# A step of the expert mixture is issued behind a deferred projection instead of behind the scores

## The chip, the cores and the metric

The kernel runs on one core of a Trainium2 chip. The metric is the device time of one execution in microseconds (us). The engines are TensorE (PE: matmuls; PEld: its weight loads), VectorE (DVE), ScalarE (ACT), GpSimd (POOL) and SyncE (SP, which only issues transfers). Each works through its own queue in order.

## The reference, cut to what matters

A layer with eight sequences of 512 tokens and 512 features. With `xn` the layer norm of `x`:

```python
s = attention(xn)          # 16 heads, chunks of 128, decay masks, carried states,
                           # gate and group norm, then @ Wo
g = silu(moe(xn))          # 16 experts, the 4 best of each token, and a shared expert
return x + s * g
```

In `moe`, every token's result is the sum of four weighted expert rows and of the shared expert's row times a sigmoid.

## The kernel before, in words

The work is in three stages. First norms, routing, the shared expert and the attention of sequences 0 and 1; then the routed experts, whose rows go to a DRAM table `y_d`; then the attention of sequences 2 to 7 (`FIRST` = 2), beside which the expert rows are gathered and mixed. The change is in this last stage.

One sequence there (`sequence`, L857) goes through four groups of four heads. For each group, in the order of the code: `scores` (L703: states, scores, VectorE's masking `sc<-ps,dmask` L750), the key of the next but one group (`key`, L678: a matmul `pk`, silu `sk` on ScalarE, and on VectorE a shuffle and three products and sums, L671 to L675), `by_token` (L684: transposes of the next key), one or two tiles of the *deferred* projection of the sequence before (`project_tiles`), the query (`query`, L681: as the key, matmul `pq`), and `output` (L755: matmuls `po`, product L776). The projection `pw` (L817) is finished by `last` (L1350): VectorE multiplies `m` by `pw` out of PSUM (L1363), then GpSimd adds `x` (L1367, `xo<-xo,m`) and SP stores it. Group 0 finishes tiles 0 and 1 of the sequence before, group 1 tiles 2 and 3.

PSUM banks come by tag; `pw`, `pq`, `po` and odd value tiles share tag "d", which has two banks. So the second `pw` of a group waits for the bank of the first, which L1363 on VectorE empties.

Between these pieces stand calls of `step()`, which is `advance` (L1384). Each call moves every active mixture tile by one piece. A tile (`mixture`, L1312) consists of four gathers by GpSimd (L1325, one per call), the addition of the first two rows (L1331, GpSimd), the addition of the other two (L1334, GpSimd) with `m<-m,sg,yg` (L1336, VectorE), `m<-m,yg` (L1340, VectorE) and a silu (L1343, ScalarE). A new tile is begun in 5 of 11 calls. Tiles of sequences 0 and 1, whose attention result waits in DRAM, end in `last` at once (there L1363 reads `m<-m,s`). The GpSimd addition of `last` is held in a list `late` and issued by a later call:

```python
while late and late[0][0] + 1 < steps[0]:
    late.pop(0)[1]()
```

The order of each engine's queue is the order in which the code issues; `behind(engine)` pins the mixture's instructions to their place. The last sequence (7) has its own loop, `last_sequence` (L942), with its own calls of `step`.

Of the kernel before, what the change touches and what calls it, by code (L numbers as in the profile page):

```python
# [38 lines left out]
FIRST = 2  # L39
# [58 lines left out]
def tile_block(ctx: ExitStack, tc: tile.TileContext, a: dict, out: bass.AP):  # L98
# [496 lines left out]
    def load_xT(b, pool=None):  # L595
        xT = (pool or home(b)).tile([P, KC, N], F32, tag="xT", name=f"xT_{b}", bufs=1)
        nc.sync.dma_start(xT.rearrange("p k n -> p (k n)"), xT_d[b])
        xT_of[b] = xT
# [10 lines left out]
    def value(b, t):  # L609
        if t == 0:  # L610
            v_of[b] = att.tile([P, NC, D], F32, tag="v", name=f"v_{b}", bufs=2)
        pv = bank("d" if t % 2 else "m", f"pv_{b}_{t}")
        for k in range(KC):
            with on_pe():
                nc.tensor.matmul(  # L615
                    pv, lhsT=xT_of[b][:, k, t * P : (t + 1) * P], rhs=wv[:, k, :],
                    start=(k == 0), stop=(k == KC - 1))
            between[0]()
        nc.scalar.copy(v_of[b][:, t, :], pv)
# [4 lines left out]
    def gate_1(b):  # L624
        pg1 = bank("a", f"pg1_{b}")
        with on_pe():
            for k in range(KC):
                for t in range(NC):
                    nc.tensor.matmul(
                        pg1[t * Q : (t + 1) * Q, :P], lhsT=wg1[:, k, :],  # L630
                        rhs=xT_of[b][:, k, t * P : (t + 1) * P],
                        start=(k == 0), stop=(k == KC - 1))
        g1_of[b] = att.tile([P, P], F32, tag="tmp", name=f"g1_{b}", bufs=TMP)
        nc.scalar.copy(g1_of[b], pg1[:, :P])

    def gate_2(b, tiles=range(NC), banks="aaaa"):
        if 0 in tiles:
            on_of[b] = home(b).tile([P, G, N], F32, tag="on", name=f"on_{b}", bufs=1)
        g1 = g1_of[b]
        p2s = {t: bank(banks[t], f"p2_{b}_{t}") for t in tiles}  # L640
        with on_pe():
            for g in range(G):
                for t in tiles:
                    tq = slice(t * Q, (t + 1) * Q)
                    nc.tensor.matmul(
                        p2s[t][:, g * P : (g + 1) * P], lhsT=wg2[tq, g * P : (g + 1) * P],
                        rhs=g1[tq, :], start=True, stop=True)
        for t in tiles:
            nc.scalar.activation(
                on_of[b][:, :, t * P : (t + 1) * P],  # L650
                p2s[t].rearrange("p (g n) -> p g n", n=P), AF.Sigmoid)
        if NC - 1 in tiles:
            g1_of.pop(b)
# [24 lines left out]
    def key(b, g, ps=None):  # L678
        kT_of[g] = rotated(b, g, "k", wk, ps)

    def query(b, g):  # L681
        qT_of[g] = rotated(b, g, "q", wq)

    def by_token(b, g):  # L684

        if not kept:
            kept.append(bank("k", f"pk_{b}_{g}"))
        pk = kept[0]
        with on_pe():
            for c in range(NC - 1):  # L690
                nc.tensor.transpose(
                    pk[:, c * P : (c + 1) * P], kT_of[g][:, c * C : (c + 1) * C], ident)
        kd = scr[0].tile([P, NC - 1, HG, HD], F32, tag="kd", name=f"kd_{b}_{g}")
        by_chunk = pk[:, : (NC - 1) * P].rearrange("p (c h d) -> p c h d", c=NC - 1, d=HD)
        for j in range(HG):
            nc.scalar.activation(
                kd[:, :, j, :], by_chunk[:, :, j, :], AF.Copy,
                scale=dk[:, g * HG + j : g * HG + j + 1])
        kd_of[g] = pk[:, (NC - 1) * P :], kd
# [55 lines left out]
    def output(b, g):  # L755
        po = bank("d", f"po_{b}_{g}")
        st, qd, sc = st_of.pop(g), qd_of.pop(g), sc_of.pop(g)
        with on_pe():
            for c in range(1, NC):
                if carry:  # L760
                    nc.tensor.matmul(  # L761
                        po[:, c * C : (c + 1) * C], lhsT=st[:, c - 1, :], rhs=qd[:, c - 1, :],
                        start=(c == 1), stop=False)
                for j in range(0 if carry else HG):
                    hs = slice(j * HD, (j + 1) * HD)
                    nc.tensor.matmul(
                        po[hs, c * C : (c + 1) * C], lhsT=st[hs, c - 1, :], rhs=qd[hs, c - 1, :],
                        start=(c == 1), stop=False)
            for c in range(NC):
                for j in range(HG):  # L770
                    h = g * HG + j
                    nc.tensor.matmul(  # L772
                        po[j * HD : (j + 1) * HD, c * C : (c + 1) * C],
                        lhsT=v_of[b][:, c, h * HD : (h + 1) * HD],
                        rhs=sc[j][:, c], start=False, stop=(c == NC - 1))
        nc.vector.tensor_tensor(on_of[b][:, g, :], po, on_of[b][:, g, :], ALU.mult)  # L776
# [16 lines left out]
    def inverse(b):  # L793
        nc.vector.reciprocal(rs_of[b], rs_of[b])
# [18 lines left out]
    def project(b, t):  # L813
        pw = bank("d", f"pw_{b}_{t}")
        with on_pe():
            for g in range(G):
                nc.tensor.matmul(  # L817
                    pw, lhsT=on_of[b][:, g, t * P : (t + 1) * P], rhs=wo[:, g, :],
                    start=(g == 0), stop=(g == G - 1))
        return pw  # L820
# [36 lines left out]
    def sequence(b, step, projected, before=None, defer=False, also=lambda: None):  # L857


        n = b + 1  # L860

        def project_tiles(q, ts):
            if q is not None:
                for t in ts:
                    projected(q, t, project(q, t))


        fill = ([0], [1], [2], [3], [], [], [], [])
        for g in range(G):
            scores(b, g)  # L870
            late_step = b == 0 and g + 2 >= G
            if not late_step:
                step()
            if g + 2 < G:
                key(b, g + 2)
            else:
                value(n, 2 * (g - 2))
            if late_step:
                step()
            if g + 1 < G:  # L880
                by_token(b, g + 1)
            project_tiles(before, fill[2 * g])
            step()
            if g + 2 < G:
                query(b, g + 2)
                if g + 3 == G and n not in xT_of:
                    load_xT(n)
            if g + 2 == G:
                value(n, 1)
            if g == 0 and b not in on_of:  # L890
                gate_2(b)
            project_tiles(before, fill[2 * g + 1])
            if fill[2 * g + 1] == [NC - 1]:
                on_of.pop(before, None)
            output(b, g)
            if defer and g + 2 == G:
                gate_1(n)
            step()
        v_of.pop(b)
        if n == FIRST:  # L900
            for _ in range(4):
                next(filling)
            gate_1(n)
            next(filling, None)
            for e in range(E - LATE // 2, E):
                nc.sync.dma_start(wexp[:, e, :], a["experts"][:, e, :])
            squares(b)
            inverse(b)
            value(n, 3)
            normed(b)  # L910
            experts_of_blocks()
            return
        if defer:
            gate_2(n)
        value(n, 3)
        also()
        squares(b)
        step()
        inverse(b)
        key(n, 0)  # L920
        also()
        query(n, 0)
        normed(b)
        also()
        if not defer:
            step()
        key(n, 1)
        by_token(n, 0)
        if defer:
            step()  # L930
        query(n, 1)
        also()
        if not defer:
            gate_1(n)
            project_tiles(b, [0, 1])
            also()
            project_tiles(b, [2, 3])
            also()
            on_of.pop(b)
        step()  # L940
# [156 lines left out]
    along()  # L1097
    enter(0, along)
    sequence(0, along, spill, also=lambda: next(sorting, None))
    for _ in sorting:  # L1100
        pass
# [14 lines left out]
    next(filling)  # L1116
    between[0] = lambda: next(filling, None)
    sequence(1, lambda: None, spill)
    between[0] = lambda: None
    slot = slots[0]  # L1120
# [354 lines left out]
```

## Time and profile before

| | us |
|---|---|
| median of three timed runs | 1143.45 (1142.99 to 1148.04) |
| profiled execution, its own time | 1133.33 |
| its span, first to last instruction | 1131.5 |
| TensorE busy in the span | 1109.5 (98%) |
| VectorE busy | 753.3 (67%) |
| GpSimd busy | 446.2 (39%) |
| ScalarE busy | 427.6 (38%) |
| granted TensorE clock, mean | 0.997 of full speed |

The last stage runs from about 690 us to the end. Within it, sequences 3 to 6 have their first group from about 761, 835, 911 and 986 us on (the matmuls `ps` of L725). A timeline line gives start, duration, engine, line, operation, what is written and read, how many instructions were merged, and in brackets the idle time ahead of it and who ended it.

### The profile page before, as it was taken

The page shows a single profiled execution, that of the slowest core. Times are in us where ns is not written, and L with a number is a line of the kernel's source. Part 1 is how long each engine was busy: PE and PEld are TensorE (multiplying, and loading weights), DVE is VectorE, ACT ScalarE, POOL GpSimd, SP SyncE. Part 2 cuts the span into 40 slices and gives each one's busy share as a digit, 9 for nine tenths or more (in the row PEclk, how much of TensorE's full clock was granted, in tenths as well). Part 3 has the DMA queues.
Part 4 walks back from the last instruction along what each step waited for, and adds up shares of the span by engine and source line. Part 5 has one row for each costly group of instructions (what it writes and reads, how often), then busy time and mean ns, then how long its engine had stood idle before and what let it go on. Part 6 is the DMA issues. An engine that isn't in the chain of part 4 may idle for free. (4 is left out here: it accounts for less than half of the span.)

```text
span 1131.5 us, 21658 instructions
## 1 busy us (share of the span) xinstructions
PE 1109.5 (98%) x7838; PEld 682.4 (60%) x7838; DVE 753.3 (67%) x1608; ACT 427.6 (38%) x924; POOL 446.2 (39%) x430
## 2 busy tenths in 40 slices
PE   7999999999999999999999999999999999999998
PEld 4445554455577777777777885655645545546453
DVE  6357744998354455555555666978789597797774
ACT  3223525255433333333333442352432523423541
POOL 4312100200333333333332314836868858768111
PEclk9999999999999999999999999999999999999999
DMA  9895341192779999999999986714648537444012
GB/s 343 311 334 187 138 161 48 57 378 88 215 208 237 236 234 238 234 239 239 241 238 267 245 203 244 270 57 160 232 121 258 156 114 250 138 138 143 11 38 75
DMA packets 163932, 218.50 MB, mean 193 GB/s; under 512 B 89840, under 2 KB 99184, under 8 KB 161776
## 3 DMA queue, kind: packets, MB, share of 16 engines
q1 hardware_dynamic: 142704, 146.76, 42.0%
q0 software_dynamic: 21120, 70.34, 24.2%
q8 instruction: 64, 1.05, 0.4%
q14 instruction: 44, 0.36, 0.1%
HBM read 126.78 MB, written 72.43 MB: 176 GB/s over the span
## 5 line engine op out<-in xcount | busy, mean ns | idle before, releaser
L1226 PE MATMUL pgu<-xts,wst 128*128 128x256 f32 x896 | 202.6, 379 | 0.0
L1226 PEld LDWEIGHTS pgu<-xts,wst 128*128 128x128 f32 x896 | 170.1, 190 | 46.2 <-issue 13.4
L1325 POOL DMA_INDIRECT yg<-y_d,place x128 | 141.6, 1106 | 30.3 <-issue 19.1
L1157 POOL DMA_INDIRECT more<-xn_d,slot x69 | 65.5, 949 | 220.1 <-DVE w L1210 107.5
L1241 PE MATMUL py<-wexp,slb 128*128 x272 | 129.9, 593 | 0.0
L1245 DVE TENSOR_SCALAR y<-py,w 128x512 f32<-128x512 f32 x136 | 102.0, 751 | 41.8 <-PE py L1241 35.4
L615 PE MATMUL pv<-wv,xT 128*128 128x512 f32 x256 | 118.3, 603 | 0.0
L659 PE MATMUL pk<-xT,wk 128*128 128x512 f32 x256 | 118.1, 603 | 0.0
L659 PE MATMUL pq<-xT,wq 128*128 128x512 f32 x256 | 115.7, 593 | 0.5 <-PEq L1289 0.5
L1232 ACT ACTIVATE slb<-pgu 128x256 f32<-128x256 f32 (+1 forms) x80 | 28.1, 351 | 219.8 <-PE pgu L1226 216.4
L817 PE MATMUL pw<-wo,on 128*128 128x512 f32 x224 | 102.3, 604 | 5.1 <-DVE m L1363 4.3
L1157 POOL DMA_INDIRECT xg<-xn_d,slot x67 | 63.6, 949 | 98.8 <-DVE w L1210 44.0
L1233 DVE TENSOR_TENSOR slb<-slb,pgu 128x256 f32<-128x256 f32 (+1 forms) x80 | 30.5, 381 | 105.3 <-ACT slb L1232 101.4
L1367 POOL TENSOR_TENSOR xo<-xo,m 128x512 f32<-128x512 f32 x31 | 45.6, 1470 | 134.2 <-DVE m L1363 126.7
L1208 DVE COPY wst<-wexp 128x512 f32 x160 | 61.7, 426 | 41.0 <-DVE y L1245 24.5
L1190 ACT COPY xts<-pl 128x512 uint16<-128x512 uint16 x110 | 84.3, 769 | 0.3 <-DMA pl<-xg 0.2
L659 PEld LDWEIGHTS pq<-xT,wq 128*128 128x128 f32 x256 | 47.2, 190 | 54.4 <-issue 53.0
L750 DVE TENSOR_TENSOR sc<-ps,dmask 128x512 f32<-128x512 f32 x128 | 79.0, 676 | 0.9 <-PE ps L725 0.9
L659 PEld LDWEIGHTS pk<-xT,wk 128*128 128x128 f32 x256 | 46.2, 189 | 50.7 <-issue 48.3
L615 PEld LDWEIGHTS pv<-wv,xT 128*128 128x128 f32 x256 | 45.9, 190 | 49.7 <-issue 46.7
L817 PEld LDWEIGHTS pw<-wo,on 128*128 128x128 f32 x224 | 41.8, 193 | 55.5 <-issue 46.2
L734 ACT COPY blocked<-state 32x96 f32<-32x96 f32 x96 | 30.8, 321 | 83.0 <-DVE state L729 82.2
(193 smaller groups left out, 1728.4 us busy)
## 6 DMA issues: line engine op xcount, KB each, us to landing
y_d<-y SPq DMA_DIRECT2D x136, 256.0 KB
wexp<-in_experts SPq DMA_DIRECT2D x16, 768.0 KB
sh_d<-sh SPq DMA_DIRECT2D x32, 256.0 KB
xT<-xT_d SPq DMA_DIRECT2D x8, 1024.0 KB
m<-sh_d SPq DMA_DIRECT2D x32, 256.0 KB
xo<-in_x SPq DMA_DIRECT2D x32, 256.0 KB
out<-xo SPq DMA_DIRECT2D x31, 256.0 KB
x<-in_x SPq DMA_DIRECT2D x7, 1024.0 KB
```

The source lines that it names most:

```text
L615: nc.tensor.matmul(pv, lhsT=xT_of[b][:, k, t * P : (t + 1) * P], rhs=wv[:, k, :], start=(k == 0), stop=(k == KC - 1))
L659: nc.tensor.matmul(ps, lhsT=w[:, k, g * P : (g + 1) * P], rhs=xT_of[b][:, k, :], start=(k == 0), stop=(k == KC - 1))
L750: masked[:] = [nc.vector.tensor_tensor(s, pss[j].rearrange("p (c t) -> p c t", t=C), dmask[:, g * HG + j].unsqueeze(1).to_broadcast([P, NC ...
L817: nc.tensor.matmul(pw, lhsT=on_of[b][:, g, t * P : (t + 1) * P], rhs=wo[:, g, :], start=(g == 0), stop=(g == G - 1))
L1157: nc.gpsimd.indirect_dma_start(out=row(i), out_offset=None, in_=xn_d, in_offset=bass.IndirectOffsetOnAxis(ap=slot[:, i : i + 1], axis=0))
L1190: (nc.vector.tensor_copy if j in by_dve else nc.scalar.copy)(xt[:, u, KP:, :].bitcast(U16).rearrange("p k (t h) -> p h k t", h=2), pls[j % ...
L1208: nc.vector.tensor_copy(to, wflat[:, bass.ds(off + u * KC * F, KC * F)])
L1226: nc.tensor.matmul(pg[:, o * n * P : (o + 1) * n * P], lhsT=wst[j % 2][k // KP][:, (k % KP * 2 + o) * F :][:, :F], rhs=xt[:, :, k, :], sta ...
L1241: nc.tensor.matmul(py, lhsT=hT[:, u * P : (u + 1) * P], rhs=wflat[:, bass.ds(off + KC * 2 * F, D)], start=True, stop=True)
L1245: gone.append(nc.vector.tensor_scalar(y, py, w[:, u : u + 1], None, ALU.mult).ins)
L1325: nc.gpsimd.indirect_dma_start(out=yg, out_offset=None, in_=y_d, in_offset=bass.IndirectOffsetOnAxis(ap=place[:, r, g : g + 1], axis=0))
L1367: nc.gpsimd.tensor_tensor(xo, xo, m, ALU.add)
```

## The change

In group 0 of sequences after the first of the stage (`b > FIRST and g == 0`), the `step()` that stood between `scores` and `key` is left out, and one is called behind `project_tiles` of that group's first tile instead, directly ahead of the `step()` that was there already. The number of calls is the same. Since `late` counts calls, the GpSimd addition that belongs to this projected tile is now issued by the second of the two calls and no longer by the call behind `output`.

```diff
         for g in range(G):
             scores(b, g)
             late_step = b == 0 and g + 2 >= G
-            if not late_step:
+            behind_tile = b > FIRST and g == 0
+            if not late_step and not behind_tile:
                 step()
             if g + 2 < G:
                 key(b, g + 2)
...
             if g + 1 < G:
                 by_token(b, g + 1)
             project_tiles(before, fill[2 * g])
+            if behind_tile:
+                step()
             step()
```

## The prediction

> **What bounds the kernel now.** I read the busy times first, then the chain of work that ended last, then TensorE's waits, and last the timelines of the places where it waits. The page's first line says that TensorE is busy for 98% of the span, so nothing can be won except where it stands idle or runs slowly.
>
> ```profile
> PE 1109.5 (98%) x7838; PEld 682.4 (60%) x7838; DVE 753.3 (67%) x1608; ACT 427.6 (38%) x924; POOL 446.2 (39%) x430
> ```
>
> The waits of TensorE from 690 us to the end (total us, times, longest) show the whole stock of idle time in the stage that the change touches: 6.0 us, of which 4.3 us stand ahead of a projection's matmuls (pw), for a VectorE product m<-m,pw (L1363).
>
> ```profile
> PE pw L817 <- DVE m L1363: 4.3, 4, 1.9
> PE pr L786 <- ACT on L649: 0.9, 1, 0.9
> PE pb L968 <- DVE on L973: 0.4, 1, 0.4
> PE pk L691 <- DVE state L729: 0.4, 1, 0.4
> ```
>
> TensorE's timeline places them. Three of the four are ahead of the second deferred projection of the first group of heads, in sequences 4, 5 and 6 (1.14, 1.13 and 1.91 us); the fourth, 0.15, stands at 865.75 ahead of the last projection of sequence 4. In sequence 3 there is none: pw follows pq at 772.80 without a gap.
>
> ```profile
> 848.10 3.70 PE L817 MATMUL pw<-wo,on 128*128 128x512 f32 x8 [1.14 <-DVE m L1363]
> 923.93 3.70 PE L817 MATMUL pw<-wo,on 128*128 128x512 f32 x8 [1.13 <-DVE m L1363]
> 1001.48 5.40 PE L817 MATMUL pw<-wo,on 128*128 128x512 f32 x8 [1.91 <-DVE m L1363]
> ```
>
> The third pw takes 5.40 us for the 3.70 of the others. The granted clock says why (columns: window, busy time and instructions of each engine, then PEclk): in the 3.41 us behind that wait TensorE had half its clock.
>
> ```profile
> 999.25:1002.66 3.41, 1.50 (x4) 0.68 (x4) 3.38 (x8) 1.20 (x2) 1.16 (x1) 1.00 0.61 204
> 1002.66:1006.07 3.41, 3.41 (x5) 1.35 (x4) 3.38 (x4) 0.02 (x1) 3.08 (x4) 0.50 0.42 125
> ```
>
> Why TensorE waits: banks "d" are two, and the second pw needs the one that VectorE empties with m<-m,pw of the first. VectorE's queue in sequence 4 has no gap there:
>
> ```profile
> 843.09 0.68 DVE L1363 TENSOR_TENSOR m<-m,s 128x512 f32<-128x512 f32 x1
> 843.69 0.74 DVE L1336 SCALAR_TENSOR_TENSOR m<-m,sg,yg 128x512 f32<-128x512 f32 x1
> 844.36 0.01 DVE L671 LOAD_MASK_SELECT swk<-sk  x1
> ...
> 847.36 0.68 DVE L1363 TENSOR_TENSOR m<-m,pw 128x512 f32<-128x512 f32 x1
> 847.96 0.69 DVE L1340 TENSOR_TENSOR m<-m,yg 128x512 f32<-128x512 f32 x1
> ```
>
> The first pw had ended at 843.36. The bank waited four microseconds for its turn in the queue, behind two instructions of the mixture and the four that make the key.
>
> **The change, part by part.** It adds and removes no instruction. In the built streams it acts in four sequences (3 to 6), not five: the last one has a loop of its own that is untouched. TensorE's order is the same throughout.
>
> *VectorE.* The mixture instructions that stood between the scores' masking and the key now stand behind m<-m,pw. By the distance from start to start: sequence 3, one m<-m,yg, 0.61 us (767.29 to 767.90); sequence 4, m<-m,s and m<-m,sg,yg, 1.27 (843.09 to 844.36); sequence 5, one m<-m,sg,yg, 1.72 (918.94 to 920.66); sequence 6, one m<-m,sg,yg, 0.67 (997.53 to 998.20). So the bank comes free that much earlier. Sequence 3 gains nothing, for there is no wait. Sequence 4 can lose its wait of 1.14, sequence 5 its 1.13, and in sequence 6 1.91 − 0.67 = 1.24 remain. Direct gain: 1.14 + 1.13 + 0.67 = 2.94 us.
>
> *What is late next.* VectorE's work is not less, only later, and its queue stays gapless up to the next thing TensorE wants from it. In sequence 4 that is m<-m,pw at 865.01 (the wait of 0.15); in sequence 5 the state scan at 934.19, for which the transposes waited 0.36. If VectorE reaches these points at the same time as now, a TensorE that is 1.1 us early waits 1.1 us more there and all is given back. So sequence 4 gains between 0 and 1.14 + 0.15 = 1.29, sequence 5 between 0 and 1.13 + 0.36 = 1.49. Which, depends on how often VectorE is stretched by GpSimd's additions: kT<-kT,swk took 2.04 at 835.32 instead of 0.69 beside an addition that began at 835.53. Eight additions between 833 and 865 stretch VectorE by 1.35, 0.45, 0.45, 1.37, 0.41, 0.70, 0.86 and 1.36, or 0.87 each. The change puts GpSimd later (next paragraph), so about one addition should slide past the return point of sequence 4: I take 0.9. In sequence 5 the last addition ahead of the return point, at 932.21, stretched its neighbour by 0.41 (m<-m,sg,yg 1.15 for 0.74): I take 0.4.
>
> In sequence 6 nothing is given back: behind the second pw VectorE itself waits (0.51 for pw at 1006.91, 1.15 and 2.78 for ScalarE at 1014 and 1021). The 0.67 stays.
>
> *The clock.* Its two halvings inside the program each lasted 3.41 us and followed a wait: 1.91 us at 999.57 to 1001.48, and 1.37 us at 234.96 to 236.33. Waits of 1.13 and 1.14, each inside one such stretch, brought none. The 1.24 that I leave in sequence 6 is between these rows and nearer to 1.14, so I take the halving as gone: 3.41 × 0.5 = 1.71 us. Bounds: 0 and 1.71. [...] The trace decides: 1.91 and 1.37 were enough.
>
> *GpSimd.* In each of the four places the addition xo<-xo,m (L1367), which waits for m<-m,pw, comes two or three instructions earlier. What it overtakes ran under its wait and now stands behind it: 3.50 us in sequence 3 (743.22 to 746.72: gather, addition, gather), 4.05 in sequence 4 (834.15 to 838.20), 2.25 in sequence 5 (917.92 to 920.17), 2.59 in sequence 6 (996.51 to 999.10). What waits for these are m<-m,sg,yg and m<-m,yg on VectorE, a step or two later: the addition at 835.53 has its reader at 854.61. I cost this at nothing; the cover is that distance, and GpSimd's own later waits, in which it catches up.
>
> *ScalarE and SP.* In sequences 5 and 6 one silu of m goes behind the key's silu and the four scalings; sk, at 917.20 held by that silu, comes up to 1.6 us earlier, but VectorE takes it at 918.94 at the soonest. Nothing. On SP five to ten loads and stores of 256 KB change places by a few positions; their readers are microseconds off. Nothing.
>
> *Sum:* 0 + 0.9 + 0.4 + 0.67 + 1.71 = 3.68 us, so a profiled span of 1131.5 − 3.7 = 1127.8. The profiled execution took 1133.33 in all, the median of the timed runs is 1143.45; I can't explain those 10 us and take the gain over unchanged: **1139.8 us**.
>
> **Rivals.**
>
> *VectorE gives it all back.* For it: from 826.87 to 865.01 the chain of waits runs through VectorE alone. Sequences 4 and 5 give 0, and the 1.24 left in sequence 6 still halves the clock: only 0.67 is gained, 1142.8. Against it: some of the stretching is moved out.
>
> *Everything is gained.* The key, being earlier, takes all four waits with it, the one of sequence 6 and its halved clock too: 1.29 + 1.49 + 1.91 + 1.71 = 6.40, so 1137.0. Against it: in sequence 6 only 0.67 is moved, unless stretching ahead of it falls away as well.
>
> *Slower: GpSimd loses its lead.* Place: m<-m,sg,yg at 819.54, where VectorE already waits 3.42 us for a GpSimd addition. If the 3.50 lost in sequence 3 is not made up by then, VectorE has 1.27 + 1.48 + 0.26 = 3.01 of idle time behind it to absorb it, and 0.49 reaches sequence 4's bank: a wait of 1.63, over the 1.37 that halved the clock, so 0.49 + 1.71 = 2.2 us lost and 1145.7. If nothing is ever made up, sequences 5 and 6 follow, and it may be 1152. It decides from the point where GpSimd makes up less than 0.49 of its 3.50. Against it: between 773 and 819 it waits 1.45 + 0.57 + 1.29 = 3.31 us.
>
> **How the numbers follow.** Forecast (gain of 2 to 5 us) 0.40; given back 0.22; all gained 0.18; slower 0.20. About 0.5%, 5.7 us, is what a measurement of this kernel can tell from no change: faster than that lies only in most of "all gained", 0.14; slower only in the upper half of the last rival, 0.09; within, 0.77. The range reaches from 1136.5 to 1146.0 and leaves out a tail of "all gained" (0.06) and the accumulating losses (0.13).
>
> **What would show it.** Right: the wait ahead of pw in the first group is gone in sequences 4 and 5 and about 1.2 in sequence 6; clock 1.00 throughout 999 to 1007; TensorE's waits for L1363 sum to 1 to 3 us. Given back: the same sum at pw of the next group or at the transposes. Wrong: new waits for GpSimd's additions longer than 3.4 us ahead of m<-m,sg,yg, or a halved clock at new places.

## The result and the profile after

The changed kernel took 1150.53 us (median of ten runs, 1147.78 to 1154.88) against 1143.54 (1141.36 to 1150.13) for the kernel before: a ratio of 1.0057 [1.0038, 1.0076]. It is slower by some 7 us, where a gain of 3.7 was forecast, and it lies outside the range. In the changed file the lines behind the edit stand three further down (L1363 is L1366 there, L1331 is L1334, L1336 is L1339, L1367 is L1370, and so on). The files of the experiments differ from these by up to three lines more.

The profiled execution took 1147.78 us, its span 1146.0. The page's first line, of the kernel after:

```profile
PE 1115.7 (97%) x7838; PEld 685.6 (60%) x7838; DVE 758.0 (66%) x1608; ACT 428.5 (37%) x924; POOL 444.0 (39%) x430
```

The profile of before that the prediction read is a poor neighbour for it: its execution took 1133.33 us, ten less than the runs' median. The kernel before was therefore profiled again (run e1_before: 1141.19 us, span 1139.4). All comparisons below are with that profile, whose line reads:

```profile
PE 1113.5 (98%) x7838; PEld 684.6 (60%) x7838; DVE 754.0 (66%) x1608; ACT 428.1 (38%) x924; POOL 446.5 (39%) x430
```

The span is 6.6 us longer. TensorE's idle time (span less busy) went from 25.9 to 30.3, 4.4 us of it; its busy time rose by 2.2 with the same 7838 matmuls. TensorE's waits from 690 us to the end (total us, times, longest) name the idle part. In e1_before:

```profile
PE pw L817 <- DVE m L1363: 2.7, 3, 1.1
PE pk L714 <- issue: 2.5, 5, 1.2
PE ps L725 <- issue: 1.9, 9, 0.2
```

And in the kernel after:

```profile
PE pk L714 <- issue: 3.3, 6, 1.2
PE pk L691 <- DVE state L729: 3.2, 1, 3.2
PE pw L817 <- DVE m L1366: 2.5, 2, 2.1
```

Three things are to be read here. The waits ahead of the projections did not go (2.7 to 2.5 us). A single wait of 3.2 us is new, ahead of the transposes of L691, for VectorE's state scan of L729. And both kernels have waits "issue", which the first profile of before did not show at all; they are small gaps inside bursts of small matmuls, and come last in this document.

The length of each sequence, from the first `ps` matmul of its first group to that of the next sequence, tells where the time is (us, from the matmuls of the trace):

| kernel | seq 2 | seq 3 | seq 4 | seq 5 | seq 6 |
|---|---|---|---|---|---|
| before, first profile | 60.62 | 73.99 | 75.84 | 75.97 | 79.67 |
| e1_before | 63.43 | 74.58 | 81.19 | 77.16 | 76.91 |
| after | 63.57 | 75.94 | 82.65 | 80.54 | 76.74 |

Against e1_before, sequence 5 is 3.4 us longer, sequences 3 and 4 some 1.4 each, sequence 6 no longer.

**Sequence 5.** Here is TensorE's timeline there (start, duration, engine, line, operation, number merged, and in brackets the idle time ahead), in the kernel after:

```profile
941.93 3.70 PE L659 MATMUL pk<-xT,wk 128*128 128x512 f32 x8
948.82 0.90 PE L691 MATMUL pk<-ident,kT 128*128 128x128 f32 x3 [3.19 <-DVE state L729]
949.52 4.61 PE L817 MATMUL pw<-wo,on 128*128 128x512 f32 x8
```

The transposes take 0.90 us for e1_before's 0.51 and the projection 4.61 for 3.60: at the end of this wait of 3.19 us the clock fell to half. The granted clock by windows (us, busy time and instructions of PE, PEld, DVE, ACT, POOL, then PEclk, DMA share and GB/s), in the kernel after:

```profile
944.50:948.10 3.60, 1.13 (x3) 0.19 (x1) 3.60 (x3) 0.00 (x0) 3.28 (x3) 1.00 0.61 187
948.10:951.50 3.40, 2.68 (x6) 1.65 (x7) 3.40 (x7) 2.62 (x9) 3.22 (x3) 0.51 0.96 354
951.50:955.00 3.50, 3.50 (x9) 1.57 (x9) 3.46 (x8) 0.90 (x3) 0.27 (x1) 0.99 0.52 151
```

VectorE is busy for all of it, so it was not waiting: it was slow. Its timeline at this place, in e1_before, from the product that empties the bank of the later projection to the state scan:

```profile
940.29 0.67 DVE L1363 TENSOR_TENSOR m<-m,pw 128x512 f32<-128x512 f32 x1
940.89 0.55 DVE L744 TENSOR_TENSOR qd<-qT,dq 128x384 f32<-128x384 f32 x1
941.36 0.68 DVE L776 TENSOR_TENSOR on<-po,on 128x512 f32<-128x512 f32 x1
941.96 1.15 DVE L1336 SCALAR_TENSOR_TENSOR m<-m,sg,yg 128x512 f32<-128x512 f32 x1
943.03 0.34 DVE L729 TENSOR_TENSOR_SCAN state<-carry,pk 128x96 f32<-128x96 f32 x1
```

The same five instructions in the kernel after:

```profile
941.97 0.67 DVE L1366 TENSOR_TENSOR m<-m,pw 128x512 f32<-128x512 f32 x1
942.56 3.25 DVE L744 TENSOR_TENSOR qd<-qT,dq 128x384 f32<-128x384 f32 x1
945.74 0.68 DVE L776 TENSOR_TENSOR on<-po,on 128x512 f32<-128x512 f32 x1
946.34 2.17 DVE L1339 SCALAR_TENSOR_TENSOR m<-m,sg,yg 128x512 f32<-128x512 f32 x1
948.43 0.34 DVE L729 TENSOR_TENSOR_SCAN state<-carry,pk 128x96 f32<-128x96 f32 x1
```

Two of them are stretched: `qd` from 0.55 to 3.25 and the mixture's sum from 1.15 to 2.17, 3.72 us together. `on`, whose operand `po` is in PSUM, is not: 0.68 in both, in e1_before beside an addition, in the kernel after beside a gather. GpSimd's timeline says what they ran beside. In e1_before:

```profile
926.74 0.97 POOL L1325 DMA_INDIRECT yg<-y_d,place  x1 [0.15 <-POOL xo L1367]
927.73 1.27 POOL L1331 TENSOR_TENSOR yg<-yg,yg 128x512 f32<-128x512 f32 x1
932.79 1.64 POOL L1367 TENSOR_TENSOR xo<-xo,m 128x512 f32<-128x512 f32 x1 [3.78 <-DVE m L1363]
...
941.04 1.52 POOL L1367 TENSOR_TENSOR xo<-xo,m 128x512 f32<-128x512 f32 x1 [1.24 <-DVE m L1363]
942.71 1.24 POOL L1325 DMA_INDIRECT yg<-y_d,place  x1
```

In the kernel after:

```profile
934.39 1.71 POOL L1370 TENSOR_TENSOR xo<-xo,m 128x512 f32<-128x512 f32 x1 [4.48 <-DVE m L1366]
...
942.89 2.50 POOL L1370 TENSOR_TENSOR xo<-xo,m 128x512 f32<-128x512 f32 x2
945.55 1.11 POOL L1328 DMA_INDIRECT yg<-y_d,place  x1 [0.16 <-issue]
946.67 1.28 POOL L1334 TENSOR_TENSOR yg<-yg,yg 128x512 f32<-128x512 f32 x1
```

In e1_before GpSimd did a gather and an addition (926.74, 927.73) while it had nothing better to do, waited 3.78 us for the first projected tile, and later waited another 1.24 for the second. In the kernel after, the first tile's addition stands ahead of that gather and that addition; they slide behind it, the later wait of 1.24 is used up by them, and in the last stretch ahead of the state scan there are three additions (two `xo`, one `yg`) where there was one.

### The profile page after: what moved, and what is told of

Its sections match the earlier page's. It is cut to its first block, busy times and chain, and to the rows that moved or that the text cites. A ratio compares the mean times of both kernels' runs of the same rounds, so it can differ in the third digit from the quotient of the medians.

```text
span 1146.0 us, 21658 instructions
## 1 busy us (share of the span) xinstructions
PE 1115.7 (97%) x7838; PEld 685.6 (60%) x7838; DVE 758.0 (66%) x1608; ACT 428.5 (37%) x924; POOL 444.0 (39%) x430
## 3 DMA queue, kind: packets, MB, share of 16 engines
q8 instruction: 64, 1.05, 0.4%
## 5 line engine op out<-in xcount | busy, mean ns | idle before, releaser
L1328 POOL DMA_INDIRECT yg<-y_d,place x128 | 139.2, 1087 | 30.4 <-issue 20.3
L1370 POOL TENSOR_TENSOR xo<-xo,m 128x512 f32<-128x512 f32 x31 | 44.1, 1425 | 151.2 <-DVE m L1366 143.9
```

What stands on the lines that cost most here:

```text
L1328: nc.gpsimd.indirect_dma_start(out=yg, out_offset=None, in_=y_d, in_offset=bass.IndirectOffsetOnAxis(ap=place[:, r, g : g + 1], axis=0))
L1370: nc.gpsimd.tensor_tensor(xo, xo, m, ALU.add)
```

## The experiments

The theories. **P**: the loss comes from GpSimd's order, the addition of L1367 that is issued one call earlier. **V**: it comes from VectorE's order, the mixture's instructions that stand behind the projection. A second question is whether the gaps in the bursts of small matmuls come from the change or with the chip. The ratios are to the kernel before on the same chip, of five rounds each.

### First runs: the two parts apart

e1_before is the kernel before again, e2_after the changed one. e3_old_add is the changed kernel with the addition put off to its old call; VectorE's and ScalarE's order is that of the change, GpSimd's that of before but for one pair in sequence 4:

```diff
+            hold[0] = int(behind_tile)
             project_tiles(before, fill[2 * g])
+            hold[0] = 0
...
-            late.append((steps[0], add))
+            late.append((steps[0] + hold[0], add))
```

e4_add_only is the other half: the kernel before with `hold[0] = -int(b > FIRST and g == 0)`, so that only the addition comes earlier. In sequence 4 this changes nothing: there the addition of a mixture tile (behind `m<-m,s`) stands ahead of it in `late` and holds it to its old call, and the trace has GpSimd's order of before. So e4_add_only has the early addition in sequences 3, 5 and 6.

> The kernel before once more, for a second profile of it: its first profiled execution (1133.33 us) was 10 us under the median of its timed runs, and the profile of the changed kernel (1147.78) shows 0.4 to 1.4 us gaps inside the bursts of small matmuls (L714, L725, L629) that the first profile of before does not show. Theory A (the gaps are a varying cost of this kernel that the first profile happened to be without): this profile shows gaps in the bursts, some 10 us in all, and the time is about 1143. Theory B (the gaps come with the change): no gaps again, profiled time near 1133 to 1143. Ratio 1.000 in both.

> The changed kernel once more, for a second profile. All theories: about 1150, ratio 1.004 to 1.008. Theory A: the gaps inside the bursts stand at other places or sum to another figure than in the first profile; theory B: at the same places with the same sum of some 15 us.

> The changed kernel, but the addition of the first projected tile (L1367 of before) is issued by the call it had before; so VectorE's and ScalarE's order is that of the changed kernel, GpSimd's that of before but for one pair of additions in sequence 4. Theory P (GpSimd loses its lead because the addition, which waits for VectorE, stands ahead of gathers): the loss is gone, ratio 0.995 to 1.000. Theory V (VectorE's new order costs the time: what stood ahead of the key now delays the query and the next group's states): ratio stays at 1.004 to 1.008.

> The kernel before, with only the addition of the first projected tile issued one call earlier, so that GpSimd has the order of the changed kernel but for one pair in sequence 4 and VectorE that of before. Theory P: ratio 1.004 to 1.008, as the whole change. Theory V: ratio 0.999 to 1.001.

| run | median, us | ratio to before (1142.89) |
|---|---|---|
| e1_before | 1142.99 | 1.0007 [0.9984, 1.0030] |
| e2_after | 1150.51 | 1.0077 [1.0054, 1.0100] |
| e3_old_add | 1141.66 | 0.9992 [0.9977, 1.0006] |
| e4_add_only | 1148.38 | 1.0045 [1.0030, 1.0061] |

P stands and V falls: the addition's place alone, in three sequences, costs 5.5 us (1148.38 − 1142.89), and without it the reordered VectorE costs nothing. The wait at L691 goes with it. TensorE's waits in e4_add_only, whose VectorE order is that of before:

```profile
PE pk L714 <- issue: 4.0, 10, 0.5
PE pk L691 <- DVE state L729: 3.5, 1, 3.5
PE pw L818 <- DVE m L1366: 2.1, 2, 1.1
```

In e3_old_add there is no wait at L691. The gaps, on the other hand, are in e1_before too: 18 of over 0.3 us between 690 and 1062 us, 7.8 us in all (after: 18 and 8.7). So they did not come with the change. (A gap is counted from one matmul's start to the next, and its size is that time less the 0.1 us that such a step takes otherwise.)

### Second runs: which sequence, and which additions

f1_early5 and f2_early3 are the kernel before with the early addition in one sequence alone (`hold[0] = -int(b == 5 and g == 0)`, and `b == 3`). f3_later is the changed kernel with the addition put off by two calls (`hold[0] = 2 * int(behind_tile)`). f4_split is the changed kernel with one single addition put off, that of tile 1 of sequence 4, which in sequence 5 stands directly beside the other `xo` (the pair of 2.50 us above):

```diff
-            late.append((steps[0], add))
+            late.append((steps[0] + int((b, t) == (4, 1)), add))
```

> The kernel before, with the addition of the first projected tile one call earlier in sequence 5 alone. Theory K (the earlier addition pushes GpSimd's next additions into VectorE's instructions that read two SBUF tensors; in sequence 5 two additions come back to back and hold qd, L744, for 3.25 us, so that the state scan is late and the transposes of the next key wait): the wait of 3 to 4 us at L691 is there, sequence 5 (first ps to first ps) is 3 to 4.5 us longer than in the kernel before, ratio 1.002 to 1.004. Theory L (GpSimd's lost lead adds up over the sequences, so one place alone does little): no wait at L691, ratio under 1.0015.

> The same in sequence 3 alone. Theory K: sequence 3 is 1 to 2 us longer, through two or three gaps of 0.65 us in the burst of L714 at the start of its second group, which all three profiles with the earlier addition have and the three without have not; ratio 1.000 to 1.002. Theory L: the loss shows in later sequences as well, ratio over 1.002.

> The changed kernel, with the addition one call later than in the kernel before (two later than in the changed one). Theory K: it depends on which of VectorE's instructions the additions meet, not on their being late as such: no pair back to back at qd, ratio 0.996 to 1.002, no wait over 2 us at L691 in sequence 5. Theory L (the more of GpSimd's work runs ahead of the waiting addition the better): ratio 0.994 to 0.998, under that of the kernel with the old call.

> The changed kernel, with one addition, that of the second projected tile of sequence 5's first group, issued one call later, so that two additions are no longer back to back at qd (L744). Nothing else differs. Theory K: qd takes about 1.9 us for 3.25, the wait at L691 falls from 3.2 to 3.8 us to 1.5 to 2.5, sequence 5 is 1.3 to 3 us shorter than in the changed kernel, ratio to the kernel before 1.003 to 1.006. Theory L: as the changed kernel, wait and ratio unchanged, 1.006 to 1.008.

| run | median, us | ratio to before (1142.31) | wait at L691, seq 5 |
|---|---|---|---|
| f1_early5 | 1145.47 | 1.0034 [1.0015, 1.0052] | 3.49 |
| f2_early3 | 1144.44 | 1.0028 [1.0010, 1.0046] | none |
| f3_later | 1142.50 | 1.0014 [0.9998, 1.0030] | none |
| f4_split | 1149.29 | 1.0069 [1.0046, 1.0092] | 3.5 |

The early addition in sequence 5 alone makes the wait of 3.49 us, and a loss of 0.34%, where the changed kernel loses 0.49 to 0.77% in its three measurements. In its profile sequence 5 is 5.8 us longer than e1_before's, more than expected, for the clock halves there twice, at 946.83 and at 974.14 (the mean granted clock of this profile is 0.993, of e1_before's 0.996). f4_split was meant to break the pair, and it did, without use. VectorE's timeline in f4_split:

```profile
949.16 2.04 DVE L744 TENSOR_TENSOR qd<-qT,dq 128x384 f32<-128x384 f32 x1
...
951.72 3.37 DVE L1339 SCALAR_TENSOR_TENSOR m<-m,sg,yg 128x512 f32<-128x512 f32 x1
955.02 0.34 DVE L729 TENSOR_TENSOR_SCAN state<-carry,pk 128x96 f32<-128x96 f32 x1
```

`qd` fell from 3.25 to 2.04, but the mixture's sum rose from 2.17 to 3.37: 5.41 us for 5.42. So my theory (K in the expectations) that the pair back to back does the harm fell. What counts, in the kernels with gathers, is how many additions of GpSimd lie between the emptied bank and the state scan. From the end of `m<-m,pw` to the scan's start, the time and the additions in it:

| kernel | us to the scan | GpSimd additions begun |
|---|---|---|
| e1_before, f2_early3 | 2.07, 2.07 | 1, 1 |
| after, e2_after, e4_add_only, f1_early5 | 5.79, 5.79, 5.79, 5.79 | 3 in each |
| f4_split, and i1_after below | 5.78, 5.78 | 3 in each |

The other profiles have one of these two values as well: of all eighteen, twelve lie at 2.06 to 2.08 us and six at 5.78 to 5.79. In the kernels with gathers, what decides between them is whether GpSimd issues the early addition in sequence 5. Without gathers (g1, g2 and i3 below) the time is 2.07 us even where the change is in (g2), although two additions begin in the stretch: the second begins only when the last product is already running (in g1 at 927.96, the product at 927.38). So an addition costs here what it holds up of the products that start behind it.

### Third and fourth runs: gathers, and the addition on VectorE

g1_plain_before and g2_plain_after replace the gathers of the kernel before and of the changed one by plain loads of SP, which leaves out the choice of rows. h1_vector_add is the changed kernel with the four `xo` additions in question on VectorE. h2_early46 was to have the early addition in sequences 4 and 6 alone; in sequence 4 it stays at its old call, as in e4_add_only, so it has it in sequence 6 alone.

```diff
-            with behind(POOL):
-                nc.gpsimd.indirect_dma_start(...)
+            i = g * TOPK + r
+            nc.sync.dma_start(yg, y_d[i * P : (i + 1) * P, :])
```

```diff
-            with behind(POOL):
-                nc.gpsimd.tensor_tensor(xo, xo, m, ALU.add)
+            first = FIRST <= b < B - 2 and t == 0
+            with behind(DVE if first else POOL):
+                (nc.vector if first else nc.gpsimd).tensor_tensor(xo, xo, m, ALU.add)
```

> The kernel before, with every gather of expert rows (L1325, 128 indirect transfers issued by GpSimd) replaced by a plain load of the same 256 KB issued by SP, rows by position instead of by index: the choice of rows is left out, bytes and additions stay. Theory G (a GpSimd gather in progress starves TensorE of instructions in bursts of small matmuls): the gaps of over 0.3 us inside bursts, 17 or 18 with 6 to 9 us in the profiles so far, fall under 1 us; time 1128 to 1137, ratio 0.986 to 0.995. Theory T (any transfer at that moment delays the refill): the gaps stay at 5 us or more, ratio 0.994 to 1.003.

> The changed kernel with the same plain loads. Theory G: no gaps in bursts, in sequence 3's second group least of all. What is left of the loss of 0.7% is the part from GpSimd's additions, whose places are others here because GpSimd has less to do: 0 to 4 us over the kernel before with plain loads. Theory T: as the changed kernel, 6 to 9 us over it.

> The changed kernel with the four additions of the first projected tile (those that moved ahead of gathers) done by VectorE instead of GpSimd, at the same place. Theory K (it is GpSimd's waiting for VectorE and the number of its additions between the bank's release and the state scan that cost): no wait at L691 in sequence 5, no gaps in sequence 3's second group, ratio 0.996 to 1.002. Theory V (VectorE's new order): loss as in the changed kernel or more, over 1.006.

> The kernel before with the early addition in sequences 4 and 6 alone, the complement of the two single places tried. Theory K: neither has a wait at L691, ratio 0.999 to 1.0015. Theory L (lost lead adds up wherever it is lost): ratio 1.002 to 1.004.

These four fell on a chip where the kernel before takes 1132.16 us and the traces of h1 and h2 hold one gap of 0.28 us each. That is how the first profile of before looks (1133.33, one gap of 0.28). I repeated four kernels on a further chip, where the kernel before takes 1143.17 again: i1_after, i2_early3 (as f2), i3_plain_before (as g1) and i4_vector_add (as h1).

> The changed kernel on another chip. If the kernel before is at 1130 to 1136 here (a chip without gaps in bursts): Theory K alone is left, a wait of 3 to 4 us at L691 in sequence 5 and its halved clock, no loss in sequence 3, ratio 1.001 to 1.005. If it is at 1140 to 1146: as so far, 1.006 to 1.009.

> The early addition in sequence 3 alone, as run once. On a chip without gaps: ratio 0.999 to 1.001 and sequence 3 at 74.0 us. On a chip with gaps: ratio 1.001 to 1.004, sequence 3 at 75.5 to 76.5.

> The kernel before with plain loads by SP in the place of GpSimd's gathers (the choice of rows by index is left out). On a chip with gaps: Theory G, gaps in bursts under 1 us, ratio 0.984 to 0.992; Theory T, gaps of 5 us or more, ratio 0.992 to 0.998. On a chip without gaps: as run once, 0.993, and nothing told apart.

> The changed kernel with the four additions of the first projected tile on VectorE, as run once on a chip where the kernel before took 1132: ratio 0.996 to 1.000 on either sort of chip.

| run | median, us | ratio to before on its chip | gaps over 0.3 us, in all |
|---|---|---|---|
| g1_plain_before | 1124.47 | 0.9927 [0.9906, 0.9948] | 0 |
| g2_plain_after | 1124.43 | 0.9930 [0.9905, 0.9956] | 0 |
| h1_vector_add | 1130.48 | 0.9979 [0.9959, 0.9998] | 1, 0.28 us |
| h2_early46 | 1132.02 | 0.9999 [0.9984, 1.0014] | 1, 0.28 us |
| i1_after | 1149.96 | 1.0049 [1.0026, 1.0071] | 18, 8.3 us |
| i2_early3 | 1143.33 | 0.9996 [0.9978, 1.0014] | 19, 7.8 us |
| i3_plain_before | 1126.37 | 0.9838 [0.9814, 0.9863] | 0 |
| i4_vector_add | 1141.19 | 0.9984 [0.9966, 1.0002] | 15, 6.7 us |

i1_after repeats the loss, if less of it than expected, and its place, on another chip. Its transposes in sequence 5:

```profile
946.85 0.90 PE L691 MATMUL pk<-ident,kT 128*128 128x128 f32 x3 [3.55 <-DVE state L729]
```

i4_vector_add has the change's VectorE order, with one addition put into it in each of the four places, and one GpSimd addition less there. The transposes of sequence 5 wait for nothing:

```profile
946.17 0.49 PE L691 MATMUL pk<-ident,kT 128*128 128x128 f32 x3
```

It takes 8.8 us less than the changed kernel beside it (1141.19, 1149.96) and, with h1, some 0.2% less than the kernel before. That is the best version with the whole computation that I ran, though one of its two intervals takes in no difference. Its longest wait in sequence 5 is another, 1.72 us ahead of the projection at 936.03.

h2_early46 loses nothing: sequence 6 tolerates the early addition, on the chip without gaps at least. What it does in sequence 4 alone, no run shows. g1 and g2 do not tell the change's halves apart, for without the gathers all of sequences 3 to 6 take 73.99 us in both, and TensorE is hardly held up.

### The rest of the loss: sequence 3

Every kernel with the early addition in sequence 3 on a chip with gaps is longer there: 75.9 to 76.4 us (after, e2, e4, f2, f4, i1, i2), against 74.5 to 74.6 in e1, e3, f1, f3 and i4. TensorE's timeline in f2_early3 shows how:

```profile
781.36 0.66 PE L714 MATMUL pk<-v,kd 128*32 128x32 f32 x18
782.46 0.28 PE L714 MATMUL pk<-v,kd 128*32 128x32 f32 x5 [0.44 <-issue]
783.19 0.21 PE L714 MATMUL pk<-v,kd 128*32 128x32 f32 x1 [0.45 <-issue]
```

The same 24 matmuls in e1_before run without a gap:

```profile
781.38 0.37 PE L714 MATMUL pk<-v,kd 128*32 128x32 f32 x24
```

Beside them GpSimd ran two gathers in f2_early3:

```profile
780.50 1.00 POOL L1328 DMA_INDIRECT yg<-y_d,place  x1 [0.30 <-issue]
781.81 0.94 POOL L1328 DMA_INDIRECT yg<-y_d,place  x1 [0.30 <-issue]
```

In e1_before it ran one addition:

```profile
780.69 1.59 POOL L1367 TENSOR_TENSOR xo<-xo,m 128x512 f32<-128x512 f32 x1 [1.45 <-DVE m L1363]
```

The early addition had pulled the gathers to where the `xo` addition stood. The price in time is less settled than the place: f2_early3 was 1.0028, above what theory K expected, and i2_early3, the same kernel, 0.9996, below it. The two intervals share 1.0010 to 1.0014, which is 1.1 to 1.6 us, and the 1.4 us of the sequence lengths lie in it; but i2 alone would also allow nothing.

## Why the prediction was wrong

**The step that failed** is the one on GpSimd: "I cost this at nothing; the cover is that distance, and GpSimd's own later waits, in which it catches up." What it overtakes was worked out rightly: 2.25 us in sequence 5 (gather and addition, 917.92 to 920.17 there, 926.74 to 929.00 in e1_before). The readers were rightly found to be far off as well. VectorE's wait for a `yg` sum stayed one long wait of 3.4 us in e1_before, in after and in e4_add_only. And GpSimd did catch up in a later wait, the 1.24 us. What I left out is that an addition of GpSimd costs something where it *runs*, not only where its result is awaited. It stretches the VectorE instruction beside it (here those with both operands in SBUF: `qd` to 3.25 us from 0.55), and the change let three of them stand, instead of one, directly ahead of a point at which TensorE waits. With the shift priced at its place, the term would have been 3.72 us on VectorE. Of these TensorE feels 3.2 to 3.5 (it had only 0.2 to 0.5 us to spare there). In four of the six profiles with this wait (after, e4, f1, i1) the clock then stood at half for 3.4 us or more (0.51 from 948.10 to 951.50 in the kernel after, 0.50 from 946.80 to 950.20 in i1_after; in e4_add_only the projection behind the wait took 5.30 us for 3.60), which adds 3.4 × 0.5 = 1.7; in e2_after and f4_split it did not fall. f1_early5, which has this term alone, measures 0.0034 × 1142.3 = 3.9 us (1.7 to 5.9).

All pieces lay in the prediction. It had the stretching (0.87 us for an addition), and it had named the state scan at 934.19 as the point where sequence 5 would be late next. It used the stretching for a gain only ("about one addition should slide past the return point of sequence 4") and never asked where the additions that slide would land.

**The rival "GpSimd loses its lead"** named the right engine and side, and was given 0.20; its mechanism did not occur. It priced the loss through a VectorE that waits for GpSimd's sums at 819.54 in sequence 4; that wait did not grow. The loss came through a VectorE that is slowed beside GpSimd, in sequence 5.

**VectorE's direct gain** of 1.14, 1.13 and 0.67 us occurred at its places, and was given back in one. In e1_before the waits ahead of the second `pw` are 1.05, 0.54 and 1.08 us in sequences 4, 5 and 6; in the kernel after, those of sequences 4 and 5 are gone. But in sequence 4 it returns doubled at the next group:

```profile
873.23 3.27 PE L817 MATMUL pw<-wo,on 128*128 128x512 f32 x7 [2.09 <-DVE m L1366]
```

That is `m<-m,pw` of the next group, the return point which the prediction named (865.01) and for which it hoped to keep 0.9. e3_old_add has the same wait, of 2.25 us, with GpSimd's old order (but for the pair of `xo`). So there, counted in waits, VectorE's own order gave back more than it gained, and the rival "given back" was right for sequence 4. Taken whole, the reordering without the early addition is worth −1.2 us on the median (e3: 0.9992), an interval that takes in no change; the forecast of 3.7 is not in it.

**The clock term** came out as forecast in the one pair of profiles that could show it, but its reason failed. On the chip without gaps h2_early46, whose VectorE order is that of before, waits 1.91 us in sequence 6 and its clock halves (the projection behind the wait takes 5.40 us for 3.70); h1_vector_add, with the order of the change, waits 1.24 us, to the hundredth what the prediction left there, and its clock does not; its sequence 6 is 2.37 us shorter, for 0.67 + 1.71 forecast. (GpSimd's order differs between the two as well.) In h2_early46:

```profile
1001.15 5.40 PE L818 MATMUL pw<-wo,on 128*128 128x512 f32 x8 [1.91 <-DVE m L1366]
```

And in h1_vector_add:

```profile
999.78 3.70 PE L817 MATMUL pw<-wo,on 128*128 128x512 f32 x8 [1.24 <-DVE m L1366]
```

The reason was that a wait's length decides, "1.91 and 1.37 were enough". That was read from one profile, and the others speak against it. The wait at 236 us is in all eighteen, 1.36 to 1.40 us long, and the clock halved behind it in four. h1_vector_add itself waits 1.83 us at 865.12, and its clock stays (1.000 in the mean of its profile). So that the halving of sequence 6 went with the 0.67 us may have been luck.

On the chips with gaps the kernel before waits only 1.08 us there. The 0.67 was won (0.41 is left in the kernel after), but there was no halving to lose (sequence 6 takes 76.91 us in e1_before, for 79.67 in the first profile), so the 1.71 could not be won in the runs that were timed.

**The 10 us** between the profiled execution and the timed median that the prediction could not explain are the gaps, as far as the traces show: on the chip where the kernel before takes 1132 us there is one, where it takes 1142 to 1143 there are 12 to 21, with 5.7 to 8.7 us. That the first profile came from a chip of the quick kind is inferred from its time and its one gap.

**What stays open.** The whole change costs 7.6 us in the first runs (e2_after) and the early addition in sequences 3, 5 and 6 alone 5.5 (e4_add_only); the intervals, 6.2 to 11.4 and 3.4 to 7.0, overlap. Whether VectorE's order, or the early addition in sequence 4, adds something once the rest is there isn't settled. The changed kernel itself wasn't run on the chip without gaps. And the 1.5 us of sequence 4 in the table are not assigned: between 79.0 and 82.9, its length changes from profile to profile with the gaps and with a halved clock at 889 to 899 us, in kernels of both kinds.

## What to carry to other kernels

When an instruction of GpSimd is moved, ask two questions: who waits for its result, and which VectorE instruction it will now run beside; the second needs no dependency and appears in no wait of VectorE (`qd` was busy for its 3.25 us). Place GpSimd's additions where VectorE has slack or reads PSUM (beside an addition its products took 1.75 us for 0.68 here with both tensors in SBUF, and 0.68 with one in PSUM), and list what lies between the last emptied bank and the next thing that TensorE takes from VectorE before anything is let into that stretch. And profile the kernel before on the chip on which the change is timed, before its idle time is counted as stock to be won: here it took 1132 us on one chip and 1142 to 1143 on three. A rule that one profile suggests, as here which waits halve the clock, should be looked for in a second one before it becomes a term of a sum.

## What the runs showed of the hardware

**VectorE beside GpSimd.** From 755 us on, in e1_before, a VectorE product with both tensors in SBUF (128x512, L673 to L675) takes 0.68 us alone, 0.68 beside a gather and 1.75 in the mean beside an addition of GpSimd (22 of them, at most 2.17); a product with an operand in PSUM takes 0.68 beside an addition as well (`on` at 941.36, beside the `xo` addition of 941.04). How the stretches sum: in f4_split, moving one addition moved the stretch from `qd` (3.25 to 2.04) to the mixture's sum (2.17 to 3.37) and left the sum alone (5.42, 5.41).

**The clock.** Waits of 1.91 us (h2_early46, where the projection behind it took 5.40 us for 3.70) and 3.19 us (kernel after, 0.51 from 948.10 to 951.50) came with 3.4 us at half clock, and so did one of 3.55 us (i1_after, 0.50 from 946.80 to 950.20); a wait of 2.09 us (873.23, kernel after) did not: the windows around it have a clock of 1.00. Nor did the waits of 3.54 us in e2_after and 3.48 us in f4_split, at the very place of the 3.19. In e2_after the instructions behind it take 0.55 and 3.60 us, for 0.90 and 4.61 in the kernel after:

```profile
951.16 0.55 PE L691 MATMUL pk<-ident,kT 128*128 128x128 f32 x3 [3.54 <-DVE state L729]
951.54 3.60 PE L817 MATMUL pw<-wo,on 128*128 128x512 f32 x8
```

The wait of some 1.37 us at 236 us was followed by half clock in four profiles of eighteen (0.50 from 238.08 to 241.49 in the first profile of before). And at 893.5 us in the kernel after the clock halved behind a burst with no gap above 0.25 us (2.59 us busy in the 3.50 ahead; 0.50 from 893.50 to 896.90). In this case, then, a wait's length by itself does not tell whether the clock falls: it fell behind 3.54 us in e4_add_only (the projection took 5.30 us for 3.60) and not behind 3.54 in e2_after, behind 1.91 and not behind 2.09.

**Gaps in bursts of small matmuls.** On three of the four chips of the experiments TensorE stalls 12 to 21 times between 690 and 1062 us, inside bursts of 24 or 32 matmuls that otherwise start some 0.01 or 0.1 us apart, mostly for 0.4 to 0.7 us each from one start to the next, "issue" in the profile. All of these stalls lie inside a gather of GpSimd or within 0.7 us of one (17 of e1_before's 18 and 16 of after's 18 begin or end inside), though gathers cover only some 35% of the bursts' time; and i3_plain_before, which has no gathers, has no stall on such a chip. It gains 16.8 us there (1143.17 to 1126.37) where the same edit gains 7.7 on the chip without gaps (1132.16 to 1124.47), and the difference, 9.1, is near what the stalls take (7.8 us in e1_before, on another chip). What in a gather does it, and what sets the chips apart, no run here shows.
